# About four hundred single pieces of a planned kernel are issued at other places of the order

## The chip, the cores and the metric

The kernel runs on one core of one Trainium2 chip. The metric is the device time of one execution, in microseconds (us). Three executions of the kernel before took 808.03, 809.57 and 809.99; their median is 809.57.

A core has five engines that work side by side, each through its own list of instructions in order: TensorE (PE, matrix products and transposes), VectorE (DVE) and ScalarE (ACT) for element-wise work, GpSimd (POOL), and SyncE (SP), which here only starts transfers. An instruction that needs another engine's result, or a buffer that another engine still reads, waits, and everything behind it on its own engine waits with it.

## The reference, cut to what matters

The input x has 16 batches of 512 rows and 512 columns, the context 16 x 512 x 1024, a mask 16 x 512, four 512 x 512 weights and some vectors, all in float32. Two residual blocks follow each other:

```python
x = x + xattn(layernorm(x), context, mask)
x = x + ffn(layernorm(x))

def xattn(e, context, mask):
    h = rmsnorm(e) * g_res @ W_in.T + b_in
    s = scan(rmsnorm(context) * g_init)     # along the rows, columns 0 to 511:
                                            # s[t] = a * s[t-1] + b * u[t], a and b constants
    return s[plug] + h                      # plug: row numbers out of running sums of the mask

def ffn(x):
    x_prev = x moved down by one row
    r = sigmoid((mu_r * x + (1 - mu_r) * x_prev) @ W_r)
    k = square(relu((mu_k * x + (1 - mu_k) * x_prev) @ W_k))
    return r * (k @ W_v)
```

So each batch needs four 512 x 512 x 512 products: `a` (W_in), `k`, `r` and `v`.

## The kernel before, in words

**Arithmetic.** TensorE gets its operands split in two: a rounded `hi` part and the rest, `lo`. Each product is made as three passes, hi·hi, hi·lo(weight) and lo·hi, that are summed in one PSUM bank (`QW`; `a_mm` L786, `gemm` L884). One pass of one 128-row tile is four matmuls of 128 x 128 by 128 x 512, in the page `MATMUL pa<-wha,xh` and so on: `pa`, `pk`, `pr`, `pw` are the banks of the products a, k, r, v, `wha`/`wla` the hi/lo weights, `xh`, `m`, `ka` the split left operands. The normalisations need no operand of their own: the row scale `rs` is applied when a bank is added to x (`a_end` L813: `x<-pa,rs,x` on VectorE), and the scaled weights of a take the layernorm's mean out.

**Per batch b**, with rows spread as p = row // 4, j = row % 4 (four tiles, j = 0 to 3):
- `load_x` (L617), `load_ctx` (L623), one per tile: transfers issued on SP. The small first loads are those of the mask and the constants `consts`, of x0 (`load_x0` L613, four) and of the weights (`load_w` L568, two halves each).
- `turn_x`/`split_x` (L629, L642): x transposed on TensorE for the batches that have it so (banks `tx`), then hi on ScalarE, lo on VectorE: `xh<-tx,xh`.
- `stat1`, `rs1` (L658, L687): mean and variance of x; the power -1/2 is taken on POOL.
- `sq`, `sq_end` (L711, L720): sums of squares of the context on ScalarE (`junk<-cx`), their power on POOL (`sq<-sq,mhalf`). `scan_u`, `scan` (L733, L748): the scan inside a row group on VectorE (`cx<-cx,sq,bc`), its carry between groups on TensorE (`pc`), and four stores of the result to a DRAM buffer `dr` (SP).
- `a_mm`, `a_end`; `gather` (L820): POOL's indirect transfers add the rows `dr[plug]` to x. `add_b` (L700) adds the bias to x, on POOL's queue.
- `norm2` (L827): the second layernorm, its statistics on VectorE (`sb<-x`), its power on POOL (`r`), y on ScalarE or VectorE. `transp` (L852): y transposed on TensorE (banks `tr`).
- `mix` (L864), for k and for r, four columns blocks each: `prev` on ScalarE, `both` on VectorE (`pv<-tr,small,pv`), hi on ScalarE, lo on VectorE or POOL.
- `k_mm`, `r_mm`, `v_mm` (L908 on): the products; relu and square of k on ScalarE or VectorE (`kr<-pk,kr`), split into `ka`; sigmoid `sg`; r times v and the sum onto x; `store` (L958) on SP.

The weights are split once, by `hi_w` and `lo_w` (L577, L581). In the first products of all (`a_first` L799, `k_first` L895) the four banks are filled side by side, one column block c at a time, so that they can begin with the first quarter of the weight. `warm` (L585) puts products of a block of ones ahead of some of them (`pa<-ones`).

**What sets the order.** `block_kernel` does not issue as it goes: `plan.add` (L74) collects 3097 numbered pieces (number n in the order of the calls; most are one to four instructions), each with the engines that may do it, an estimated cost, what it reads and writes, and the buffers that it opens. `Plan.order` (L119) then plays the whole program through on the host with these costs: at each moment every idle engine takes the ready piece with the earliest due time `late`. Due times come from `deadlines` (L90), which adds a fixed shift by stage and batch out of the table `SHIFT` (L326). A buffer is one of a fixed number of slots, `SLOTS` (L308: 3 of x, 2 of raw, 5 of cx, 16 operand pairs `op`, 8 `tmp`, and 4 + 4 PSUM banks `ps` and `tr`), and the order also says which slot each piece opens. It is a list of (planned start, engine, piece, slots).

At the end of `block_kernel` (L1258 to L1276) the list is walked once: slots become tiles, each piece's function issues its instructions on its engine through `InOrder` (L290), which keeps them in this order. So the list sets, for every engine, the sequence in which it works, and nothing else does; what an instruction waits for follows from the data and from the slots. Since all instructions go through one helper, they all have the line L300 in the profile, and are told apart by their tiles. Two waits are added in the same walk from the list's own order: a piece of POOL that uses the port shared with VectorE waits for the last such piece of VectorE that stands ahead of it (L1264 to L1269), and a load on SP waits for the last TensorE piece ahead of it whose planned end is at least `TIE` = 5 us before the load's planned start (L1270 to L1276).

Planned times are the planner's, not the chip's; only the sequence goes to the chip. In the following, "n341" is the piece with number 341, and "place" is a piece's position in its own engine's sequence, counted from 0.

Of the kernel before, what the change touches and what calls it, by code (L numbers as in the profile page):

```python
# [62 lines left out]
class Plan:  # L63
# [55 lines left out]
    def order(self):  # L119
# [7 lines left out]
        wait = [len(p.before) for p in ps]  # L127
        fixed = {e: [n for n in reversed(ORDER.get(e, ())) if n < len(ps)] for e in ENGINES}
        owned, offered = {n for v in fixed.values() for n in v}, set()
        events, out = [], []  # L130
# [17 lines left out]
        while left:  # L148
# [9 lines left out]
            while events and events[0][0] <= now:  # L158
                _, what, n, e = heapq.heappop(events)
# [13 lines left out]
            for e in ENGINES:  # L173
# [26 lines left out]
                while queue[e] and best is None:  # L200
                    item = heapq.heappop(queue[e])
# [19 lines left out]
                    for k, kinds in p.new.items():  # L221
                        for kind in kinds:
                            used = sum(1 for v in take.values() if v[0] == kind)
                            ahead = 0
# [49 lines left out]
                if p.moves:  # L274
                    first, last, _ = DMA[p.queue]
# [6 lines left out]
                heapq.heappush(events, (end if p.moves else end + HOP, 0, p.n, e))  # L282
                out.append((now, e, p, take if out else {**take, **self.given}))
        self.end = max(v for v in idle.values())
        return out

# [1 line left out]
class InOrder:  # L290
# [98 lines left out]
    ("sq", 4): 2.2,  # L389
    ("stat1", 4): 2.5,  # L390
    ("store", 4): -10.4,
    ("plugs", 8): -40.0,
    ("plugs", 12): -40.0,
}
ONLY = {
    ("rv", 0): 0,
# [38 lines left out]
NKR = 4  # L435
LATE = ()
ORDER = {}
RAW_IN = {2: ("op", "raw")}
CX_IN = {}
NLATE = 4  # L440
# [15 lines left out]
def block_kernel(  # L456
# [77 lines left out]
    def K(name, *parts):  # L534
        return [(name, p) for p in (parts or (0,))]
# [66 lines left out]
    def load_raw(b, eng=SP, early=INF, at=None):  # L602
        for h in range(2):
# [3 lines left out]
                    S[n], xT[b].rearrange("(cc p) t -> p cc t", p=P)[:, 2 * h : 2 * h + 2]),  # L607
                (), K(n), new={n: (RAW_IN.get(b, ("raw",)), [P, 2, T], F32)}, moves=1.55, early=early, at=at)

# [726 lines left out]
```

## Time and profile before

| | us |
|---|---|
| three executions | 808.03, 809.57, 809.99 (median 809.57) |
| the profiled execution, whole | 808.87 |
| its span from first to last instruction | 807.1 |
| TensorE busy | 788.4 (98% of the span) |
| VectorE busy | 594.3 (74%) |
| ScalarE busy | 486.0 (60%) |
| POOL busy | 453.1 (56%) |

The span is measured on the chip's own clock from the first to the last instruction recorded; 1.8 us of the execution lie around it. A batch takes some 47 us of it. "Granted clock" is the share of full speed that TensorE was granted; it changes in slices of 3.41 us, and in the whole execution it stands at 0.5 in two stretches after the start, from 15.08 to 21.90 and from 66.28 to 69.69 us. Full-width matmuls begin 0.233 us apart at 1.0 and 0.427 us apart at 0.5.

In the rows of a timeline: start, length, engine, line, operation, result and operands by the program's names, sizes, number of instructions joined to one row, and in brackets the idle time just before and the engine and tile that ended it.

### The profile page before, as it was taken

How to read it: one execution, taken by the hardware profiler on the slowest of the kernel's cores; microseconds unless marked ns; L12 is line 12 of the kernel's file. 1: busy time of each engine (PE TensorE's matmuls, PEld its weight loads, DVE VectorE, ACT ScalarE, POOL GpSimd, SP SyncE). 2: the span in 40 equal slices, each digit the busy share in tenths (PEclk: the TensorE clock that was granted, in tenths of full speed). 3: DMA queues.
4: the chain of work that ended last, by engine and by line, in shares of the span. 5: the costliest groups of instructions: out<-in, count | busy, mean ns of one | idle time of the engine just before them, and what ended most of it. 6: DMA issues, size and time to landing. Idle time of an engine off the chain costs nothing. (4 is left out here: it accounts for less than half of the span.)

```text
span 807.1 us, 11158 instructions
## 1 busy us (share of the span) xinstructions
PE 788.4 (98%) x3627; PEld 628.2 (78%) x3627; DVE 594.3 (74%) x1323; ACT 486.0 (60%) x950; POOL 453.1 (56%) x374
## 2 busy tenths in 40 slices
PE   7998999999999999999999999999999999999997
PEld 4776877878787888888788888878788888888885
DVE  6899798989789696785857679685866949464432
ACT  6937496655483767467566756457675664655540
POOL 2843766574767656567665556537856554661220
PEclk8999999999999999999999999999999999999999
DMA  9867586895775777667665766756786674430011
GB/s 327 270 95 262 104 220 170 288 220 160 144 234 147 179 199 206 157 209 145 212 140 171 220 157 209 157 162 152 184 234 157 209 138 171 73 89 0 9 45 52
DMA packets 52554, 134.69 MB, mean 167 GB/s; under 512 B 4752, under 2 KB 5264, under 8 KB 50576
## 3 DMA queue, kind: packets, MB, share of 16 engines
q1 hardware_dynamic: 35744, 102.39, 37.3%
q0 software_dynamic: 16608, 31.46, 24.2%
q8 instruction: 28, 0.46, 0.2%
q14 instruction: 30, 0.25, 0.1%
q10 hardware_dynamic: 144, 0.13, 0.0%
HBM read 85.73 MB, written 33.55 MB: 148 GB/s over the span
## 5 line engine op out<-in xcount | busy, mean ns | idle before, releaser
L300 POOL TENSOR_TENSOR m<-pv,m 128x512 fp32r<-128x512 f32 x86 | 120.9, 1414 | 121.3 <-ACT m L300 59.7
L300 PE MATMUL pa<-wha,xh 128*128 128x512 f32 x512 | 136.7, 404 | 5.8 <-DVE x L300 2.0
L300 PE MATMUL pw<-whv,ka 128*128 128x512 f32 x512 | 139.0, 398 | 0.0
L300 POOL DMA_INDIRECT x<-dr,plug x64 | 113.2, 1769 | 45.3 <-issue 17.0
L300 PE MATMUL pr<-whr,m 128*128 128x512 f32 x512 | 138.4, 397 | 0.0
L300 PE MATMUL pk<-m,whk 128*128 128x512 f32 x512 | 133.8, 396 | 0.6 <-DVE x L300 0.6
L300 ACT ACTIVATE pv<-tr,om 128x384 f32<-128x384 f32 (+1 forms) x256 | 100.8, 485 | 52.4 <-PE tr L300 28.5
L300 DVE SCALAR_TENSOR_TENSOR pv<-tr,small,pv 128x511 f32<-128x511 f32 x128 | 94.9, 741 | 38.7 <-ACT pv L300 37.9
L300 PEld LDWEIGHTS pa<-wha,xh 128*128 128x128 f32 x512 | 96.9, 191 | 31.9 <-DVE x L300 2.8
L300 PEld LDWEIGHTS pk<-m,whk 128*128 128x128 f32 x512 | 95.6, 188 | 24.8 <-DVE x L300 1.0
L300 PEld LDWEIGHTS pr<-whr,m 128*128 128x128 f32 x512 | 95.5, 188 | 23.0 <-DVE kr L300 0.4
L300 PEld LDWEIGHTS pw<-whv,ka 128*128 128x128 f32 x512 | 95.0, 188 | 21.8
L300 ACT CAST m<-pv 128x512 fp32r<-128x512 f32 x128 | 76.1, 642 | 37.1 <-DVE pv L300 31.8
L300 ACT ACTIVATE sg<-pr 128x512 f32<-128x512 f32 x64 | 38.1, 598 | 95.6 <-PE pr L300 88.6
L300 DVE TENSOR_TENSOR ka<-kr,ka 128x512 fp32r<-128x512 f32 x48 | 35.9, 749 | 76.3 <-ACT ka L300 76.2
L300 DVE TENSOR_TENSOR sg<-pw,sg 128x512 f32<-128x512 f32 (+1 forms) x65 | 43.9, 676 | 41.5 <-PE pw L300 41.5
L300 ACT ACTIVATE junk<-cx 128x1024 bf16<-128x1024 f32 x64 | 67.5, 1055 | 6.7 <-DMA cx<-cx 6.1
L300 PE MATMUL pa<-wla,xh 128*128 128x512 f32 x256 | 71.2, 401 | 0.3 <-POOL wla L300 0.3
L300 ACT ACTIVATE y<-x,r 128x512 f32<-128x512 f32 x48 | 38.9, 814 | 53.7 <-DVE r L300 37.4
L300 PE MATMUL pw<-wlv,ka 128*128 128x512 f32 x256 | 70.4, 397 | 0.0
L300 PE MATMUL pr<-wlr,m 128*128 128x512 f32 x256 | 70.3, 396 | 0.0
L300 PE MATMUL pk<-m,wlk 128*128 128x512 f32 x256 | 69.9, 396 | 0.0
(116 smaller groups left out, 1238.9 us busy)
## 6 DMA issues: line engine op xcount, KB each, us to landing
cx<-cx SPq DMA_DIRECT2D x64, 512.0 KB
dr<-cx SPq DMA_DIRECT2D x64, 256.0 KB
out<-x SPq DMA_DIRECT2D x31, 512.0 KB
x<-x SPq DMA_DIRECT2D x15, 1024.0 KB
x<-bc POOLq DMA_DIRECT2D x14, 1024.0 KB
raw<-xT SPq DMA_DIRECT2D x26, 512.0 KB
wsa<-winT SPq DMA_DIRECT2D x2, 512.0 KB
x<-x SPq DMA_DIRECT2D x4, 256.0 KB
```

Of the source, the lines that this page charges most:

```text
L300: r = self._tc.keep_in_program_order(op(*args, **kwargs))
```

## The change

Two things. In `SHIFT`, the stage "plugs" of batches 8 and 12 (row numbers for four batches at a time) gets -50 in place of -40, so the planner sees them due 10 us earlier. This changes the planned order between about 305 and 400, and 500 and 590 us; sixteen of the pieces that VectorE or POOL may do change sides there, eight in each direction. And a new table `MOVES` is applied to the list after planning: for each pair (n, m), piece n is taken out and put right ahead of piece m. Slots stay with the pieces, and a check sees to it that no piece comes ahead of one that it needs or of the last use of its slot. Engines, operations, sizes and planned start times of the moved pieces stay; what the two added waits take as "ahead in the list" moves with them.

```diff
@@ order()
-        return out
+        return self.moved(out) if MOVES else out
+
+    def moved(self, out):
+        item = {x[2].n: x for x in out}
+        order = [x[2].n for x in out]
+        users, owner = {}, {}
+        for n in order:
+            for k in item[n][2].names:
+                users.setdefault(k, []).append(n)
+        need = {n: set(item[n][2].before) for n in order}
+        for n in order:
+            for k, slot in item[n][3].items():
+                if slot in owner:
+                    need[n].update(users[owner[slot]])
+                owner[slot] = k
+        for n, m in MOVES:
+            order.remove(n)
+            order.insert(order.index(m), n)
+        seen = set()
+        for n in order:
+            assert need[n] - {n} <= seen, "a piece is ahead of one that it needs, or of the last use of its slot"
+            seen.add(n)
+        return [item[n] for n in order]
@@ SHIFT
-    ("plugs", 8): -40.0,
-    ("plugs", 12): -40.0,
+    ("plugs", 8): -50.0,
+    ("plugs", 12): -50.0,
@@
+MOVES = [
...
+    (362, 634), (515, 362), (624, 515), (509, 623), (513, 509), (364, 621), (601, 363), (594, 361),
+    (622, 600), (593, 598), (620, 593), (359, 620), (492, 359), (358, 492), (587, 358), (357, 360),
...
+    (405, 407), (301, 405), (404, 301), (435, 404), (403, 260), (300, 403), (400, 406), (410, 400),
...
+    (428, 420), (427, 428), (177, 427),
...
+    (372, 373), (175, 372), (349, 175), (345, 349), (347, 348),
...
+    (170, 377),
...
+    (344, 416),
+    (346, 344), (255, 343),
...
+    (341, 371),
...
+    (333, 248),
...
+    (291, 205),
...
+    (199, 237), (198, 199),
...
+    (88, 157),
...
+    (28, 30),
...
+    (106, 21), (20, 106), (19, 20), (105, 17), (6, 105), (5, 6),
...
+    (7, 4), (3, 0),
+]
```

The pairs are worked through from the first to the last; the last in the table belong to the start of the program. Places that hold another piece than before: TensorE 188 of 896, VectorE 307 of 881, ScalarE 205 of 735, POOL 89 of 367, SP 45 of 218. `MOVES` reaches from the start to about 300 us; behind 590 us the sequences are the same as before.

The pieces that the prediction names:

| piece | what it is | place before, after (engine) | time before, us |
|---|---|---|---|
| n3 | load of consts | 3, 0 (SP) | start |
| n7 | load of x0, tile 3 | last, first of the four (SP) | start |
| n28 | lo of xh0, block 0 | 15, 14 (DVE) | 13.65 |
| n106 | mean of x0's tile 3, after a sum on ScalarE | 11, 6 (DVE) | |
| n120, n121 | 29 products of ones, first pass of a0 | 13, 14 both times (PE) | 14.39, 18.27 |
| n46 | lo of W_in, block 3 | 12, 9 (POOL) | 26.55 |
| n128 | first pass of a0 with lo weights | 22 both times (PE) | 27.98 |
| n199 | lo of xh1, block 2 | 58, 54 (DVE) | 38.32 |
| n291 | lo of xh2, block 2 | 71, 68 (DVE) | 46.72 |
| n333, n248 | first passes of a2 tile 0 and a1 tile 2 | 44, 43 and 43, 44 (PE) | 47.45, 44.76 |
| n341 | end of a2, tile 1 | 103, 91 (DVE) | |
| n255 | end of a1, tile 3 | 98, 95 (DVE) | 65.03 |
| n346, n344 | first pass of a2 tile 3, a pass of its tile 2 | 64, 63 and 63, 64 (PE) | 65.82, 62.33 |
| n427 | mix for r, batch 0, block 3, `both` | 93, 105 (DVE) | 61.11 |
| n349 | end of a2, tile 3 | 105, 104 (DVE) | 70.48 |
| n386 | first pass of k0, opens the four `pk` banks | 67 both times (PE) | 71.28 |
| n276 | load of context 2, tile 0 | 26, 32 (SP) | 32.86 |
| n299, n300 | power of sq2 (POOL), first scan step of batch 2 (DVE) | n300: 124 | 82.09, 83.71 |
| n403 | square of k0, block 1 | 126, 125 (DVE) | 85.39 |
| n435 | first pass of r0, tile 1 | 87, 85 (PE) | |
| n359, n362, n365 | y2 of tiles 1, 2, 3 | 177, 182, 185 to 176, 181, 184 (DVE) | before 127.8 |

## The prediction

> **What bounds the kernel now.** I first read the busy times and the forty slices of the page.
>
> ```profile
> PE 788.4 (98%) x3627; PEld 628.2 (78%) x3627; DVE 594.3 (74%) x1323; ACT 486.0 (60%) x950; POOL 453.1 (56%) x374
> ...
> PE   7998999999999999999999999999999999999997
> ...
> PEclk8999999999999999999999999999999999999999
> ```
>
> TensorE is busy 788.4 of 807.1 us, and its low digits stand in the first slices. A new order can save only stops of TensorE, 18.7 us in all, most of it at the start. Second, busy time by stage (start and end, length, then PE, PEld, DVE, ACT, POOL with their instructions, granted clock, DMA share, GB/s):
>
> ```profile
> 0.00:16.00 16.00, 11.92 (x69) 6.49 (x70) 9.69 (x44) 8.11 (x18) 2.81 (x11) 0.97 0.88 306
> 16.00:34.00 18.00, 16.50 (x72) 12.34 (x71) 15.65 (x35) 16.47 (x40) 13.80 (x15) 0.84 0.85 305
> 34.00:72.00 38.00, 33.22 (x181) 26.17 (x180) 36.21 (x83) 24.19 (x53) 20.36 (x18) 0.96 0.73 182
> 72.00:132.00 60.00, 59.49 (x295) 46.09 (x293) 51.81 (x117) 39.49 (x81) 36.08 (x30) 1.00 0.64 172
> ```
>
> From 34 to 72 us TensorE stops for 4.8 us and VectorE is busy 36.21 of 38.00: there VectorE is the bound. From 72 to 132 TensorE stops for 0.5 us by this view and is the bound itself. Third, the timeline's stops of TensorE and what ended them.
>
> ```profile
> 47.45 1.20 PE L300 MATMUL pa<-wha,xh 128*128 128x512 f32 x4 [1.60 <-DVE xh L300]
> ...
> 65.82 1.72 PE L300 MATMUL pa<-wha,xh 128*128 128x512 f32 x4 [2.01 <-DVE x L300]
> ...
> 71.28 0.96 PE L300 MATMUL pk<-m,whk 128*128 128x512 f32 x3 [0.61 <-DVE x L300]
> ...
> 127.82 0.66 PE L300 MATMUL tr<-consts,y 128*128 128x128 f32 x4 [0.41 <-DVE y L300]
> ```
>
> Every one is ended by VectorE: n291, n255, n349 and n359. Fourth, VectorE's own rows ahead of them.
>
> ```profile
> 44.93 0.69 DVE L300 BATCH_NORM_STATS2 sb<-x 128x6 f32<-128x512 f32 x1 [0.24 <-DMA x<-dr,plug]
> ...
> 46.20 0.60 DVE L300 TENSOR_SCALAR y<-x,r 128x512 f32<-128x512 f32 x1 [0.17 <-POOL r L300]
> ...
> 65.03 0.74 DVE L300 SCALAR_TENSOR_TENSOR x<-pa,rs,x 128x512 f32<-128x512 f32 x1
> ...
> 70.48 0.75 DVE L300 SCALAR_TENSOR_TENSOR x<-pa,rs,x 128x512 f32<-128x512 f32 x1 [1.00 <-PE pa L300]
> ```
>
> VectorE stands still for 0.24, 0.17 and 1.00 us only; in the last it waits for the passes of a2's tile 3, which TensorE ran late (after its stop of 2.01) and at half clock. So those two engines wait for each other in turn, and the 1.00 goes if n255, which ended that stop, comes early enough.
>
> Fifth, the clock slices:
>
> ```profile
> 45.80:49.21 3.41, 1.81 (x9) 1.44 (x9) 3.14 (x13) 0.00 (x0) 3.24 (x4) 1.00 0.57 78
> 62.86:66.28 3.42, 1.41 (x7) 0.85 (x6) 3.42 (x8) 3.34 (x8) 2.65 (x3) 1.00 0.99 345
> 66.28:69.69 3.41, 3.41 (x10) 2.65 (x9) 3.19 (x6) 3.41 (x8) 2.35 (x2) 0.50 1.02 391
> ```
>
> The slice with 1.41 us of TensorE work was followed by one at half clock; the slice with 1.81 was not.
>
> **The change part by part.**
>
> *Start, to 34 us.* n28 moves one place up and n106 five places up, to where it waits for ScalarE and holds the boundary pieces behind it, which began at 8.33, till about 9.8. n28 ended at 14.3 and gates the 29 products of ones (n120) that began at 14.39. I let it end up to 0.85 later, at 15.15. At half clock the 29 last 29 x 0.106 = 3.1 us, to 18.3; the first pass of a0 began at 18.27, since ScalarE's n36 keeps its place. So 0. On POOL n46 moves three places up, so n128's stop of 0.45 for it can go; but n88 and n45 on VectorE come two places up too, with up to 0.2 of new waiting. 0 to -0.35, and 0 in the sum: the bound after 34 us is VectorE, and TensorE's lead is lost there. The SP moves (n3, n7) reorder transfers whose DMA share is 0.88; bounded by one x0 load's place, they can delay n28 by no more than I gave it.
>
> *34 to 72 us.* From the end of the work ahead of this stretch (42.49) to the end of n349 (71.23) VectorE spends 28.74 us. n427, 0.79 long, moves from place 93 to 105, behind n349: -0.79. The idle 0.24 + 0.17 + 1.00 = 1.41 can go: n341 moves 12 places up and n255 three, n346 goes ahead of n344, and with a shorter stop no slice at half clock follows. Together at most -2.2. New waits: n341 twelve places earlier needs a2's tile 1 whose passes are not moved as far; n152 and the four transposes are closer together. I bound what they give back by the shortest and the longest idle of VectorE ahead of this stretch's rows, 0.3 and 1.0. So n349 and k0's first pass n386 come earlier by 1.2 to 1.9; I take 1.5, nearer the low idle, as most moves carry a piece's producers with it. At TensorE: of the stops 1.60 + 2.01 + 0.61 and the eight matmuls at half clock (8 x (0.427 - 0.233) = 1.6), 1.5 go; the rest is VectorE's bound and stays.
>
> The SP queue in this stretch: n276 falls back from place 26 to 32, behind the stores of dr1, so context 2's first tile arrives some 30 us later (issued at 32.86 before, near 67 then). Its user is ScalarE's square ahead of n299, at 82.09 on POOL. n170 (second half of W_r) goes behind both halves of W_v, three pieces of ScalarE behind it with slack of over 10 us. I cost both at 0; if the cover is gone, n299 and with it n300 and n403 are late, which is the next item.
>
> *72 to 90 us.* From here TensorE has no stops to give and what it is ahead by must be kept.
>
> ```profile
> 83.71 0.75 DVE L300 SCALAR_TENSOR_TENSOR cx<-cx,sq,bc 128x512 f32<-128x512 f32 x1 [1.71 <-POOL sq L300]
> ...
> 84.98 1.10 PE L300 MATMUL pr<-wlr,m 128*128 128x512 f32 x4
> ...
> 85.39 1.28 DVE L300 SCALAR_TENSOR_TENSOR kr<-pk,kr 128x512 f32<-128x512 f32 x2
> ```
>
> n435, the first pass of r0's tile 1, is moved two places up, to the place that ran at 84.98, and needs the bank that n403 (85.39 to 86.07) empties. n403 now stands ahead of n260 (1.0), and the chain ahead of it comes up to 1.15 earlier (its share of the 1.5): it ends no sooner than 86.07 - 1.0 - 1.15 = 83.9. So TensorE keeps at most 84.98 - 83.9 = about 1.0 of its 1.5. VectorE stood still 1.71 at n300 for POOL; that wait stays where the power is taken. -1.0 for all up to here. Ends: 0 (n300's wait moves with nothing, n403 ends at 84.98 plus) and -1.5.
>
> *127 to 132 us.* Three stops for y2's tiles 1 to 3, 0.57 + 0.20 + 0.29 = 1.06 by matmul starts. n359, n362 and n365 move one place up, the load of x3 one place up on SP, and the store's inputs n462 and n467 earlier. I let all go: -1.06. Ends: -1.06 and +0.5, the longest of them doubled, because one place is 0.7 us of VectorE but n357 now stands two places later.
>
> *300 to 600 us.* The pieces of "plugs" 8 and 12 go up to 15 places up on VectorE and POOL; sixteen splits change engine, eight each way. TensorE's stops there (0.82 at 393.5, 0.70 at 583.8) are for work that is not moved. Cost +0.1, ends 0 and +0.5; the cover is the lead that VectorE has when it is busy 74%, and without it a late split costs the 1.4 us that POOL takes for one (its page row 1414 ns) less VectorE's 0.75.
>
> *Sum.* -1.0 - 1.06 + 0.1 = -1.96, taken as -1.9, on the profiled execution's 808.87: **807.0 us**. That execution lies 0.70 below the median of the three, 809.57, and 0.84 above the lowest. The ends of the terms give -2.9 to +1.0; the likeliest case, with 0.6 below for an execution's scatter and cut above where R3 begins, has 805.4 to 808.2.
>
> The Trainium skill ("TensorE: Matmul & The Clock Gate", section "HAM oscillation — how this bites in real kernels") speaks of the clock falling only after idle gaps over some 3.4 us. Here a stop of 2.01 us was enough, as the slices above show, so the measurement decides. By the page no stop here would cost a half-clock slice and the 1.00 us of VectorE idle would not be tied to one; the sum would then be 806.9 + 1.0 = 807.9, against 807.0 by the rows.
>
> **The rivals.**
>
> R1, more than summed: VectorE's idle between 20 and 34 us (0.45 + 0.29 + 0.76 + 0.70 = 2.2) goes as well, and what is won is kept through 84 us. For it: VectorE is the bound until 72 us, and each idle there is worth its length. Against: n435 at its new place. 808.87 - 4.1 = 804.8. Chance 0.22.
>
> R2, the other side: the clock. The order spreads TensorE's stops, and two more slices of 3.41 us fall under the 1.81 us of work that was enough to stay at full clock. Each then runs 9 or 10 matmuls where 16 ran at full clock (x9 and x16 in the slices of 18.49 and 21.90 us), 7 x 0.233 = 1.6 us. 808.87 + 3.2 = 812.1, if the order's gain is lost too. It decides from a stop of some 1.6 to 2.0 us that VectorE does not hide, near 48 or 66 us. Against it: both known stops get shorter by the places above. Chance 0.20.
>
> R3, the order does nothing that can be measured: the work of VectorE to 72 us is the same, and new waits take the place of the old. 808.9. Chance 0.20.
>
> **How the numbers follow.** Differences below 0.3% (2.4 us) can't be told from none, about what the executions differ by. Likeliest case 0.38, of it 0.21 faster by more than that against the median and 0.17 within; R1 0.22 faster; R2 0.18 slower and 0.02 within; R3 0.16 within, 0.02 each side. Faster 0.45, same 0.35, slower 0.20. The range reaches from R1, a little past it, to short of R2: 803.6 to 811.5; outside are the upper half of R2 and a tenth for more than R1.
>
> **What would show it.** Right: k0's first pass near 69.8 in place of 71.28; the stop before the pass of n346 under 1.6 and no slice at half clock between 60 and 75; n435 beginning around 84 with a short stop for VectorE's `kr`; no stops for `tr<-consts,y` near 127; the stretch from 300 us on as long as before. Wrong: a stop for `kr` or `sq` of over 1.5 us near 84; a new slice at half clock; stops at 350 us for splits that POOL now makes; or a start at which the first pass of a0 comes after 18.5.

## The result, and the profile after

The changed kernel is slower: median 813.77 us against 809.73 for the kernel before, eight executions each, ratio 1.0054 with a 95% interval of 1.0038 to 1.0070. By this ratio that is 4.4 us more. The forecast was 807.0.

The profiled execution after has a span of 811.1 us, 4.0 more than before's 807.1. Its page, busy times and slices (the helper's line is now L322):

```profile
PE 787.3 (97%) x3627; PEld 627.6 (77%) x3627; DVE 600.1 (74%) x1323; ACT 486.2 (60%) x950; POOL 453.2 (56%) x374
...
PE   7898999999999999999999999999999999999997
...
PEclk9999999999999999999999999999999999999999
```

TensorE does the same work (787.3 against 788.4); VectorE is busy 5.8 us longer with the same 1323 instructions. Busy time by stage after (start and end, length, PE, PEld, DVE, ACT, POOL with instructions, granted clock, DMA share, GB/s):

```profile
34.00:72.00 38.00, 32.73 (x183) 25.26 (x182) 37.41 (x83) 22.86 (x50) 22.92 (x19) 1.00 0.71 172
72.00:132.00 60.00, 58.44 (x291) 45.66 (x290) 51.73 (x115) 41.16 (x85) 36.02 (x29) 1.00 0.68 190
132.00:165.00 33.00, 33.00 (x156) 26.18 (x155) 29.54 (x61) 20.84 (x44) 19.02 (x14) 1.00 0.81 239
165.00:208.00 43.00, 38.98 (x181) 30.34 (x180) 37.47 (x81) 22.38 (x45) 21.66 (x19) 0.96 0.61 166
208.00:300.00 92.00, 90.88 (x405) 72.69 (x405) 72.66 (x148) 56.44 (x110) 64.75 (x50) 1.00 0.72 186
300.00:600.00 300.00, 299.89 (x1365) 242.24 (x1364) 228.53 (x514) 187.45 (x358) 183.89 (x150) 1.00 0.67 180
```

The same view of before, from 132 us on:

```profile
132.00:165.00 33.00, 32.90 (x155) 26.51 (x156) 30.48 (x61) 19.81 (x40) 20.51 (x14) 1.00 0.84 239
165.00:203.00 38.00, 37.92 (x184) 29.99 (x183) 35.34 (x82) 22.41 (x47) 21.52 (x18) 1.00 0.70 187
203.00:300.00 97.00, 95.50 (x423) 75.77 (x423) 78.79 (x157) 59.09 (x114) 65.92 (x53) 1.00 0.71 182
```

One row stands out. From 165 to 208 us TensorE stops for 4.0 us; before, it stopped for 0.1 from 165 to 203. The prediction had no row for this stretch. TensorE's stops in the timeline after, with what ended them:

```profile
46.37 2.13 PE L322 MATMUL pa<-wha,xh 128*128 128x512 f32 x8 [1.27 <-DVE xh L322]
...
62.80 1.19 PE L322 MATMUL pa<-wha,xh 128*128 128x512 f32 x4 [0.98 <-DVE x L322]
...
70.07 3.40 PE L322 MATMUL pk<-m,whk 128*128 128x512 f32 x12 [1.41 <-DVE x L322]
...
83.14 0.94 PE L322 MATMUL pr<-ones 128*128 128x128 f16 x14 [0.54 <-ACT kr L322]
...
85.37 1.20 PE L322 MATMUL pr<-whr,m 128*128 128x512 f32 x4 [0.31 <-DVE kr L322]
...
169.91 1.19 PE L322 MATMUL pk<-m,whk 128*128 128x512 f32 x4 [1.03 <-DVE cx L322]
...
190.96 0.24 PE L322 MATMUL cp<-ohj,oh 128*128 128x4 f16 x4 [1.34 <-DVE sg L322]
...
204.45 1.20 PE L322 MATMUL pk<-m,whk 128*128 128x512 f32 x4 [1.65 <-DVE sg L322]
```

Up to 72 us the two stops that the prediction named first got shorter (1.27 for 1.60, 0.98 for 2.01), and the one at k0 got longer (1.41 for 0.61). In the stretch from 34 to 72 us TensorE stops for 5.3 us in all, against 4.8 before. The first pass of k0 came at 70.07; compared matmul by matmul, TensorE is 0.65 us ahead of before there. Then the stops at 83.14 and 85.37 give that back. In this execution the loss falls between 165 and 208 us: the three stops from 169.91 to 204.45 sum to 4.0. The slice that holds the stop at 190.96 (189.08 to 192.49) was followed by one at a granted clock of 0.54:

```profile
189.08:192.49 3.41, 2.07 (x23) 1.32 (x22) 3.38 (x6) 1.31 (x5) 0.00 (x0) 1.00 0.00 1
192.49:195.90 3.41, 3.41 (x16) 2.31 (x13) 2.51 (x9) 2.99 (x8) 0.33 (x1) 0.54 0.88 300
```

What VectorE did ahead of 204.45 is the find of the case. Its timeline after holds one addition of 2.94 us, on n843, which before took 0.69:

```profile
199.29 2.94 DVE L322 TENSOR_TENSOR x<-x,sg 128x512 f32<-128x512 f32 x1
```

POOL's timeline after, at the same time, two splits back to back (n944 and n948):

```profile
198.48 3.19 POOL L322 TENSOR_TENSOR m<-pv,m 128x512 fp32r<-128x512 f32 x2
```

And before, VectorE and then POOL:

```profile
195.41 0.69 DVE L300 TENSOR_TENSOR x<-x,sg 128x512 f32<-128x512 f32 x1
```

```profile
196.28 2.75 POOL L300 TENSOR_TENSOR m<-pv,m 128x512 fp32r<-128x512 f32 x2
```

Before, the splits begin after n843 has ended at 196.10. After, they run beside it, and n843 ends at 202.23, 0.56 behind n948's end at 201.67.

This does not come from a change of sequence. n843 and the splits stand in the same order on their own engines in both kernels. It is one of the two waits that the emission loop takes from the list: a piece of POOL that uses the shared port waits for the last such piece of VectorE **ahead of it in the list**. Two pairs of the table, (948, 842) and (944, 948), put n944 and n948 ahead of n842 and n843. So n944 no longer waits for n843.

### The profile page after: what moved, and what is told of

Read it like the earlier page. It is cut to its first block, busy times and chain, and to the rows that moved or that the text cites. A ratio compares the mean times of both kernels' runs of the same rounds, so it can differ in the third digit from the quotient of the medians.

```text
span 811.1 us, 11124 instructions
## 1 busy us (share of the span) xinstructions
PE 787.3 (97%) x3627; PEld 627.6 (77%) x3627; DVE 600.1 (74%) x1323; ACT 486.2 (60%) x950; POOL 453.2 (56%) x374
## 4 chain that ended last, share of the span: by engine, by line
PE 71%; DVE 12%; DMA 7%; ACT 4%; issue 4%; POOL 1%; SPq 0%; DVEq 0%; ACTq 0%; POOLq 0%
PE pr L322 19%; PE pw L322 17%; PE pk L322 16%; PE pa L322 15%; DMA cx<-cx 3%; PE tr L322 3%; DVE x L322 3%; DVE cx L322 3%; DVE pv L322 2%; DMA x<-dr,plug 2%; ACT junk L322 2%; DVE sg L322 1%; DMA dr<-cx 1%; PE pc L322 1%; DMA x<-x 1%
## 5 line engine op out<-in xcount | busy, mean ns | idle before, releaser
L322 POOL TENSOR_TENSOR m<-pv,m 128x512 fp32r<-128x512 f32 x86 | 119.9, 1418 | 105.4 <-ACT m L322 61.7
L322 POOL DMA_INDIRECT x<-dr,plug x64 | 114.5, 1789 | 47.8 <-DMA x<-bc 19.1
L322 PE MATMUL pr<-whr,m 128*128 128x512 f32 x512 | 139.5, 399 | 1.5 <-ACT xh L322 0.7
L322 PE MATMUL pw<-whv,ka 128*128 128x512 f32 x512 | 139.6, 400 | 0.0
L322 PE MATMUL pa<-wha,xh 128*128 128x512 f32 x512 | 134.2, 398 | 5.3 <-ACT wha L322 1.7
L322 PE MATMUL pk<-m,whk 128*128 128x512 f32 x512 | 133.9, 396 | 4.3 <-DVE sg L322 1.6
L322 ACT ACTIVATE pv<-tr,om 128x384 f32<-128x384 f32 (+1 forms) x256 | 100.4, 482 | 44.6 <-PE tr L322 23.2
L322 DVE SCALAR_TENSOR_TENSOR pv<-tr,small,pv 128x511 f32<-128x511 f32 x128 | 94.9, 741 | 36.9 <-ACT pv L322 36.9
L322 PEld LDWEIGHTS pa<-wha,xh 128*128 128x128 f32 x512 | 95.4, 188 | 30.1 <-DVE x L322 2.6
L322 PEld LDWEIGHTS pk<-m,whk 128*128 128x128 f32 x512 | 95.4, 187 | 29.9 <-issue 2.2
L322 PEld LDWEIGHTS pr<-whr,m 128*128 128x128 f32 x512 | 95.4, 189 | 24.8 <-ACT xh L322 1.1
L322 PEld LDWEIGHTS pw<-whv,ka 128*128 128x128 f32 x512 | 95.4, 189 | 22.4 <-DVE cx L322 0.4
L322 ACT CAST m<-pv 128x512 fp32r<-128x512 f32 x128 | 76.4, 640 | 39.3 <-DVE pv L322 38.2
L322 DVE TENSOR_TENSOR ka<-kr,ka 128x512 fp32r<-128x512 f32 x52 | 39.5, 759 | 79.9 <-ACT ka L322 79.8
L322 ACT ACTIVATE sg<-pr 128x512 f32<-128x512 f32 x64 | 38.3, 598 | 98.9 <-PE pr L322 90.0
L322 ACT ACTIVATE y<-x,r 128x512 f32<-128x512 f32 x48 | 39.1, 815 | 60.9 <-DVE r L322 46.0
L322 DVE TENSOR_TENSOR sg<-pw,sg 128x512 f32<-128x512 f32 (+1 forms) x65 | 44.0, 678 | 39.5 <-PE pw L322 38.9
L322 ACT ACTIVATE junk<-cx 128x1024 bf16<-128x1024 f32 x64 | 67.5, 1055 | 8.3 <-DMA cx<-cx 7.8
L322 PE MATMUL pw<-wlv,ka 128*128 128x512 f32 x256 | 70.4, 397 | 0.0
L322 PE MATMUL pr<-wlr,m 128*128 128x512 f32 x256 | 70.4, 397 | 0.0
L322 PE MATMUL pa<-wla,xh 128*128 128x512 f32 x256 | 70.0, 397 | 0.0
L322 PE MATMUL pk<-m,wlk 128*128 128x512 f32 x256 | 69.9, 396 | 0.0
```

The costliest lines, as they stand in the source:

```text
L322: r = self._tc.keep_in_program_order(op(*args, **kwargs))
```

## The experiments

The list can be cut where both orders have placed the same set of pieces: at its places 427, 665 and 905, which TensorE passes at about 99, 152 and 214 us in the trace of before (the expectations have 104 and 154 for the first two). Between cuts either order can be taken. Ratios are to the kernel before, of executions on the same chip, six to twelve for each run and 24 to 29 of the kernel before, with 95% intervals; 0.1% is 0.81 us.

**One part at a time** (e1 to e4). The edit, with its range in each run; `out` is the planner's list, and with -40.0 it is that of before:

```diff
-        return [item[n] for n in order]
+        return [item[n] if any(a <= k < b for a, b in KEEP) else out[k] for k, n in enumerate(order)]
+KEEP = ((0, 427),)         # e2: ((427, 665),)   e3: ((665, 905),)   e4: ((905, 1274),)
-    ("plugs", 8): -50.0, ("plugs", 12): -50.0,
+    ("plugs", 8): -40.0, ("plugs", 12): -40.0,    # e4 keeps -50.0
```

> Only the first 427 places of the list (to about 104 us on the chip) in the new order. In the trace of the changed kernel TensorE reaches the end of this part 0.6 us later than before, though its stops up to 90 us are 0.3 us shorter in sum. Theory 1 (the loss is made in the third part, where VectorE is 92% busy): no change that can be told, -0.3 to +0.8 us. Theory 2 (the order of the start leaves VectorE late, and that is what costs later): +2 to +4 us, with stops of TensorE for VectorE near 168 and 190 us. My forecast for this part was -1.0.

> Only places 427 to 665 (about 104 to 154 us) in the new order. Theory 1: -1.1 to 0 us by itself: the three stops for y2 near 127 us (1.06) go, a stop of 0.86 near 121 comes. At 154 us VectorE should be 0.5 to 0.9 us behind before's time, as in the changed kernel. Theory 2: this lateness alone gives stops over 1 us near 169 and 190 us, +2 to +4.

> Only places 665 to 905 (about 154 to 214 us) in the new order. In the changed kernel TensorE falls from 0.2 to 5.5 us behind here. Theory 1 (the order within this part does it): +3 to +5.5 us, with the stop near 190 us for VectorE's sg, one near 204, and VectorE's addition x<-x,sg held for 2 to 3 us next to POOL's splits. Theory 2 (it takes VectorE's lateness from the parts ahead): 0 to +1.5. Theory 3 (the slice at half clock near 193 us is chance): +1.5 to +2.5 less where no such slice falls.

> Only the places from 905 on (from about 214 us) in the new order, the earlier row numbers (plugs) included. In the changed kernel the lag falls from 5.5 to 4.06 us in this part, mainly by the two stops at 393.5 and 583.8 us (0.82 and 0.70) that are gone. Both theories: -1.0 to -1.5 us.

| part in the new order | ratio | interval |
|---|---|---|
| e1: first | 1.0038 | 1.0022 to 1.0053 |
| e2: second | 0.9989 | 0.9977 to 1.0000 |
| e3: third | 1.0040 | 1.0024 to 1.0056 |
| e4: rest | 0.9991 | 0.9977 to 1.0005 |

The third part costs 3.2 us without any lateness from ahead: in its trace TensorE enters the part 0.2 us early and leaves it 4.2 late, with the same stops and again 2.93 us for n843. So theory 2, lateness handed on, fell for this part. But theory 1 did not expect the first part's +3.1. Its trace has a stop that the changed kernel has in a smaller size, near 84 us (TensorE):

```profile
84.39 0.94 PE L322 MATMUL pr<-ones 128*128 128x128 f16 x14 [2.28 <-ACT kr L322]
```

ScalarE in the same run, the last square of context 2 and then the relu n398, which frees k0's first bank:

```profile
82.71 1.06 ACT L322 ACTIVATE junk<-cx 128x1024 bf16<-128x1024 f32 x1 [1.10 <-DMA cx<-cx]
...
83.77 0.58 ACT L322 ACTIVATE kr<-pk 128x512 f32<-128x512 f32 x1
```

Before, the relu waited for TensorE itself:

```profile
82.56 2.07 ACT L300 ACTIVATE kr<-pk 128x512 f32<-128x512 f32 x4 [3.20 <-PE pk L300]
```

In the new order n276 is loaded with the three others of context 2, after 69 us, and the squares n295 to n297 end 3 to 4.5 us later than before (79.27 before, 83.77 here, 82.52 in the changed kernel). The relu stands behind them.

**Three suspects out, each alone and all** (e5 to e8). The edits to the table, on the third part (e5, e6), the first part (e7) and the whole change (e8):

```diff
-    (948, 842), (944, 948),       # e5, e8
-    (826, 849),                   # e6, e8
-    (276, 221),                   # e7, e8
```

> The third part alone in the new order, but the moves of n944 and n948 (two of POOL's splits) ahead of n842 and n843 are left out. No engine's sequence differs from the run of the third part; only the wait for the turn at the port does: POOL's n944 waits for VectorE's n843 again. Theory 1a (the two moves take this wait away, and then VectorE's n843 is held beside POOL's splits): n843 takes 0.7 us in place of 2.9, the stop near 203 us for n960 (1.58) goes, and of the 3.3 us that the third part costs 1.4 to 1.8 go, which leaves +1.5 to +1.9 to before. Rival (n843 was held by something else, or the stop is covered by the next wait): +2.8 to +3.8 as the third part.

> The third part alone, but without the one move that puts n826 (a pass of r2) behind the counting products n657; two places of TensorE are exchanged against the run of the third part. Theory 1b (TensorE stands at n657 for the bank that VectorE's n837 frees, with n826 ready behind it, and the slice with this stop is followed by one at half clock): the stop of 1.54 near 188 us falls to 0.3 to 0.7, no slice at half clock follows (1.3), and 1.0 to 2.5 of the 3.3 us go: +0.8 to +2.3 to before. Rival (the stop comes back for the next piece that needs VectorE): +2.8 to +3.8.

> The first part alone in the new order, but n276 (load of context 2, tile 0) keeps its old place on SP (26 in place of 32); nothing else differs from the run of the first part. Theory 2a (four loads of context 2 are now issued together after 69 us, their squares on ScalarE wait for them, and the relu n398 that frees k0's bank stands behind these squares): n297 ends 1.2 to 2.5 us earlier, the stop of 2.43 near 82 to 84 us falls to 0.2 to 0.7, and the first part costs -1.0 to +1.3 us against before in place of +2.9. Rival (the squares wait for something else, the later stops near 128 us are what the part costs): +2.0 to +3.3.

> The whole change without these three: n944 and n948, n826 and n276 stay where they were. If theories 1a, 1b and 2a hold and add up, 4.4 us slower becomes -1.5 to +0.8 us against before. If the lost time goes to other waits: +2 to +4.

| run | ratio | interval |
|---|---|---|
| e5: third part without n944, n948 | 1.0011 | 0.9996 to 1.0026 |
| e6: third part without n826 | 1.0061 | 1.0040 to 1.0082 |
| e7: first part without n276 | 1.0022 | 1.0007 to 1.0037 |
| e8: whole change without all three | 1.0001 | 0.9988 to 1.0014 |

e5 takes 0.29% off the third part without changing any engine's sequence; n843 is back to 0.69 us. What is left, +0.9 us, is less than the 1.5 to 1.9 that theory 1a expected. e6 fell to its rival, and +4.9 us is above that rival's range too. By matmul starts, TensorE's stop at n657 shrank from 1.54 to 0.63, but one of 1.13 came for the next counting product n661, whose input VectorE makes later, and the stop at n960 grew from 1.58 to 2.83. e7 took the stop at 84 us away; its ratio is 0.16% (1.3 us) below e1's, with intervals that overlap, and +1.8 us lies between the ranges of theory 2a and its rival. e8 shows that the three hold the whole loss, not which of them.

**The turn alone, and the change without it** (e9 to e12). e9 is the kernel before with a table of two pairs; e10 and e11 are the whole change without the turn's pairs and without n276's; e12 has the second part and the rest.

```diff
 e9:  MOVES = [(948, 842), (944, 948)], plugs at -40.0
 e10: MOVES without (948, 842), (944, 948)
 e11: MOVES without (276, 221)
 e12: KEEP = ((427, 665), (905, 1274))
```

> The kernel before with only n948 and n944 moved ahead of n842 in the list. No engine's sequence changes; POOL's n944 no longer waits for VectorE's n843. Theory 1a by itself (the lost wait is enough): n843 is held to 2.9 us, a stop of 1 to 2 us at n960, +1.5 to +2.5. Theory 1a with a condition (n843 must also be late against POOL, as it is in the changed kernel where n666 waits for the counting products): in the trace of before n843 ends at 196.10 and n944 begins at 196.28 after a gather's issue, so they do not meet, and the time stays within -0.6 to +0.6.

> The whole change, only with n944 and n948 left in their old places of the list: no engine's sequence differs from the changed kernel. By the runs of the third part (+3.3 with the moves, +0.9 without) 1.5 to 2.4 of the 4.4 us go: +2.0 to +2.9. If the other two moves carry the loss: +3.7 to +4.8.

> The whole change, only with n276 in its old place on SP. By the runs of the first part (+3.1 with the move, +1.8 without) about 1.3 of the 4.4 us go: +2.4 to +3.6. If the load was no cause, +4 to +4.8; if all that is left after the turn hangs on it, +1.5 to +2.4.

> Only places 427 to 665 and from 905 on in the new order, the earlier row numbers included: the two parts that measured -0.9 and -0.7 alone. If parts add up: -1.0 to -2.2 against before. If the stops for y2 near 127 us that the second part removes come back as lateness further on: -0.7 to +0.3.

| run | ratio | interval |
|---|---|---|
| e9: before, with the two moves alone | 1.0056 | 1.0036 to 1.0076 |
| e10: whole change without the two moves | 1.0000 | 0.9991 to 1.0009 |
| e11: whole change without n276's move | 1.0040 | 1.0025 to 1.0056 |
| e12: second part and rest | 0.9981 | 0.9969 to 0.9993 |

This settles which moves make the loss. Two pieces moved in the list, with no engine's sequence changed, cost 0.56%: of all waits that the walk takes from the list, only that of n944 for n843 differs between e9 and the kernel before, and between e10 and the changed kernel. Some four hundred other moves cost nothing in sum. e9's trace, VectorE, POOL and TensorE:

```profile
196.31 4.16 DVE L322 TENSOR_TENSOR x<-x,sg 128x512 f32<-128x512 f32 x1
```

```profile
196.72 3.19 POOL L322 TENSOR_TENSOR m<-pv,m 128x512 fp32r<-128x512 f32 x2
```

```profile
202.69 1.20 PE L322 MATMUL pk<-m,whk 128*128 128x512 f32 x4 [3.01 <-DVE sg L322]
```

And e10's, the whole change with the wait in place:

```profile
197.59 0.69 DVE L322 TENSOR_TENSOR x<-x,sg 128x512 f32<-128x512 f32 x1
```

```profile
198.46 2.53 POOL L322 TENSOR_TENSOR m<-pv,m 128x512 fp32r<-128x512 f32 x2 [1.08 <-PE pk L322]
```

```profile
200.50 1.20 PE L322 MATMUL pk<-m,whk 128*128 128x512 f32 x4 [0.44 <-DVE sg L322]
```

In e10 the splits begin at 198.46, just after n843's end at 198.28. The trace puts their wait down to another engine; that it is the turn follows from e5 and e10, which differ from e3 and from the changed kernel in nothing else.

My condition for e9, that the pieces would not meet without other lateness, was wrong, and +4.5 us is also more than the 1.5 to 2.5 that theory 1a gave the lost wait by itself. I had read n944's start at 196.28 as held by the gather's issue (194.74 to 196.44); it was held by n843's end at 196.10. In e9 n944 begins 1.09 us after the gather does, inside n843. Behind n843 on VectorE stands n847, which empties the bank that n960 needs, so the hold of 3.5 us (4.16 - 0.69) came out as a stop of 3.01.

The traces do not place the whole cost at this stop. By matmul starts TensorE loses 3.3 us there from before to e9, 1.7 from e5 to e3, and only 1.2 from e10 to the changed kernel. Between these last two profiled executions 1.2 us more had arisen by 190 us and 1.6 in the slice at half clock at 192.5, both ahead of n944. That slice is no effect of the lost wait: e5 and e8, which have the wait, show one at the same stage, and e10 and e15 do not after stops of 1.15 and 1.40 us at the same place. By ratio the lost wait costs 4.4 us in the whole change; the ends of the two intervals leave 2.3 to 6.4. Where the part of it lies that the stop at n960 does not show is open. One candidate is further slices at half clock: e9's six executions had a mean granted clock of 0.9925, the 28 of the kernel before on that chip 0.9950. One half-clock slice of 3.41 us takes 0.0021 off the mean, so that is, as an estimate, 1.2 slices more, at 1.6 us each 1.9 us. These means do not say where in the program the slices fell, and e9's own trace has its half-clock slices only ahead of 25 us, so this is not shown.

n276's move is not shown to cost or gain: e11 is 0.14% below the changed kernel, with intervals that overlap. Its +3.2 us lies in the range that I had given for the load as a part of the cause.

e12 is faster than the kernel before by 0.19% (0.07 to 0.31).

**What the other moves do together** (e13 to e15).

```diff
 e13: KEEP = ((0, 665), (905, 1274))
 e14: as e13, MOVES without (276, 221)
 e15: KEEP = ((427, 1274),), MOVES without (948, 842), (944, 948)
```

> First, second and last part in the new order, the third (places 665 to 905) as before. Against the kernel before: if the first part costs the same in company as alone (+3.1), +1.0 to +2.2, since the second and last part alone make -1.5. If its cost alone was the stops for y2 near 127 us, which the second part's order does away with, -1.5 to -0.3. If it brings the 1.0 that the forecast had for it, -3.0 to -2.0.

> As the run without the third part, but n276 in its old place on SP. If n276's load costs through the squares of context 2 (theory 2a), 0.7 to 1.5 faster than that run; if not, within 0.5 of it.

> Second, third and last part in the new order, without the two moves of n944 and n948, the first part as before. The run of second and last part was -1.5. If the rest of the third part costs nothing, -2.0 to -0.8; if the stop of 1.3 to 1.5 for the counting products n657 stays in it, -0.8 to +0.6.

| run | ratio | interval |
|---|---|---|
| e13: first, second, rest | 0.9985 | 0.9977 to 0.9994 |
| e14: the same, n276 in its old place | 0.9995 | 0.9981 to 1.0008 |
| e15: second, third without the turn's moves, rest | 1.0006 | 0.9995 to 1.0018 |

The first part, +0.38% alone, costs nothing that can be told in company (e13 against e12: 0.9985 and 0.9981). Putting n276 back gains nothing there (e14 is 0.10% slower than e13). With e7 and e11, 0.16% and 0.14% the other way and each within its noise, theory 2a, a real wait in e1's trace, is not shown as a cause of the change's loss. The rest of the third part costs 0.25% (e15 against e12: 2.0 us); e15's trace shows the stop for n657 again, 1.55 us by matmul starts.

The sum: second part and rest -1.5 us, first part about 0, the third without the turn's moves +1.2 to +2.0 (e10 against e13, e15 against e12), the turn +4.5 (e9, alone). That gives +4.2 to +5.0, against 4.4 measured.

## Why the prediction was wrong, point by point

- **The step that failed: no term for the waits that moved with the list, and none for 132 to 300 us.** The sum went from 127-132 straight to 300-600 us. I walked each engine's sequence and the buffers; the turn at the port is a third kind of order, which changed while no sequence did. It measured +4.4 us (e10 against the changed kernel) and +4.5 us by itself (e9). None of my rivals had it. The other moves of the third part had no term either; they measured +1.2 to +2.0.
- **34 to 72 us, "k0's first pass earlier by 1.2 to 1.9".** This step failed too. The last matmuls of a2 ran at full clock, as forecast, and brought TensorE 1.8 us ahead by 70 us, of which 0.7 stood already at 35 us. But k0's second matmul began at 70.64 against 71.28, 0.65 earlier: VectorE's last row for a2, which it waits for, ended at 70.58 against 71.23, not 1.2 to 1.9 earlier. VectorE before and after:

```profile
70.48 0.75 DVE L300 SCALAR_TENSOR_TENSOR x<-pa,rs,x 128x512 f32<-128x512 f32 x1 [1.00 <-PE pa L300]
```

```profile
69.18 1.40 DVE L322 SCALAR_TENSOR_TENSOR x<-pa,rs,x 128x512 f32<-128x512 f32 x2
```

  And 1.6 of the stops I counted on was a slice at half clock that is not in every execution of the order before. In e3, which has the first part as before, the same stop of 2.04 us (64.33 to 66.37) fell across the edge of two clock slices, and no slice at half clock followed:

```profile
62.11:65.53 3.42, 2.23 (x8) 1.14 (x7) 3.42 (x10) 3.31 (x8) 1.39 (x2) 1.00 1.00 335
65.53:68.94 3.41, 2.57 (x11) 2.12 (x12) 3.41 (x8) 3.41 (x8) 3.41 (x3) 1.00 0.99 368
```

  Of nine traces with that part as before, six have the slow slice and three do not. The eight traces with the new first part have none there, as forecast, but that is a gain only against executions that had one.
- **72 to 90 us, "TensorE keeps at most 1.0".** It kept nothing: r0 began at 83.14 against 83.21. I costed n276's move at nothing and named n299 as what its loss would delay. What it delayed was n398, which stands behind the squares on ScalarE. With n276 back, r0 still began at 82.8 (e7, e14). First part in company: 0 in place of -1.0.
- **127 to 132 us, -1.06.** The three stops went in the changed kernel; one of 0.86 came at 121 us. The second part alone measured -0.9 (interval -1.9 to 0). The size is uncertain because the stops are: they depend on when the gathers land. With that part as before, n367's stop was 0.41 in the profile I used, and up to 3.32 in e7 (TensorE; then VectorE's statistics ahead of it, which had waited 1.72 for the gather in the profile I used):

```profile
130.37 0.89 PE L322 MATMUL tr<-consts,y 128*128 128x128 f32 x4 [3.32 <-DVE y L322]
```

```profile
124.56 0.69 DVE L322 BATCH_NORM_STATS2 sb<-x 128x6 f32<-128x512 f32 x1 [3.97 <-DMA x<-dr,plug]
```

- **300 to 600 us, +0.1.** It came out on the other side: e4 -0.7, within its interval of no change. The stops at 393.5 and 583.8 that I said would stay are gone from the trace after (299.89 of 300 us busy).
- **R1 and R3.** Without the two moves the change comes to what R3 said, no difference that can be told (e10: 1.0000), as a sum of -1.5 and +1.2 to +2.0 us in parts that R3 did not look at; nothing of R1's larger gain showed.
- **The clock** (R2) had a part in the profiled execution, one slice at 192.5 us, behind the stop at 190.96 and not at 48 or 66 us, where R2 looked for it.

What stays open is why the first part costs 3.1 us alone. The traces of e1 and e7 have stops of 2 and 3.5 us near 127 to 130, but kernels with the old first part show 1 to 3.7 there. In company the new first part shows no stop near 127 (e13), which is what the expectation of e13 with -1.5 to -0.3 had assumed (-1.2 measured); that this is the reason was not tested by itself.

## What to carry to other kernels

Where waits are derived from the order in which a program is written out, list every such rule before costing a reorder, and ask of each moved piece which wait it gains and which it loses; a wait that is lost can cost time, here 0.56%. Compare not only each engine's own sequence but the pairs of engines that a rule orders. And cost every stretch that the moves reach, above all one where the second engine is over 90% busy. From 132 to 203 us VectorE was, and there a hold of 3.5 us came out at TensorE as a stop of 3.0 (e9). Where it has room, a hold costs little: e12, the fastest run, has one of 4.04 us at 246.36, and the next stop of TensorE is 0.44.

## What the runs showed of the hardware

- An addition of VectorE that meets two of POOL's element-wise pieces back to back (the second recorded from 0.7 us before the first's end) is held to the end of the second, not only of the first. In the five traces without the turn (the changed kernel, e3, e6, e9, e11) n843 ended 0.56 us after the second split in every one, and took 2.93 or 2.94 us, or 4.16 in e9, where it had begun 0.41 ahead of the first split. In the twelve with it, it took 0.69. POOL pays too: the two splits took 1.95 and 1.94 us in the changed kernel, 1.50 and 1.49 before, 1.29 and 1.27 in e10. Even before, a smaller case shows the same distance: n848, begun at 198.30 beside n948, ended 0.55 us after it.
- The same distance stands all over the traces. In the seventeen, 940 of VectorE's 512-column TENSOR_TENSORs with two inputs in SBUF overlap one of POOL's by the records. Each ends either 0.54 to 0.61 us after the last of POOL's that it overlaps (569) or 1.13 to 1.17 ahead of it (371).
- The Trainium skill ("SBUF — State Buffer", section "Who interferes with whom") says that a VectorE instruction with two inputs in SBUF contends with a GpSimd instruction that reads SBUF. The same page (section "🔬 SBUF: two separate sides") says that the one that starts first has the shared pair for the whole instruction while the other blocks. The holds agree with the first. On the second the runs differ in part: 27 of the 569 had begun 0.03 to 0.64 us ahead of POOL's by the records (POOL's are rough) and were still held, e9's n843 past two of POOL's instructions.
- The clock slices lie at other places of the program in every execution: counted from the program's first instruction, their edges differ by up to 2.5 us between the seventeen traces. What TensorE did within one slice goes with the clock of the next. The stop of 2.0 us near 65 us lay inside one slice in six traces, with 1.39 to 1.41 us of work left in it, and the next was at half clock. In three it fell across an edge or partly outside (least work in a slice 2.23 in e3, 2.09 in e9, 1.66 in e12), and none was. Behind the first 25 us, all ten full-clock slices with 1.51 us of work or less were followed by one at half clock, and none with 1.60 to 2.00 was. Five more such followed slices with 2.02 to 2.22 us at 188 to 195 us, where the counting products stand; a sixth there, with 2.01 in e15, was not.
